# Attention and spectral filter on one Trainium2 core: scratch for eight filter rows, a pair turned in two steps, and inverse-transform visits of two places

## The chip, the cores and the metric

The kernel runs on one core of a Trainium2 chip (trn2), all in float32. The metric is the device time of one execution in microseconds (us). Times are given as the median of several executions; in addition one execution was taken by the hardware profiler, and all views of the profile are of that one.

A core has TensorE (matrix products; PE in the profile, its weight loads PEld), VectorE (DVE), ScalarE (ACT), GpSimd (POOL) and SyncE (SP), which here only issues transfers. Each engine works through its own instructions in order. Matmuls write to PSUM, which has eight banks; VectorE and ScalarE empty it. The profile counts a float32 matmul as two records and a transpose as one.

## The reference

The input is an image batch `x` of shape (2, 128, 64, 64). A first layer (group norm, a neighbourhood attention and two small products) adds to it. The second layer, where the change lies, is this:

```python
t = _to_tokens(x)                      # (2, 4096, 128)
t = t + _L1_attn_ref(_ln_t(t))
t = t + _L1_ffn_ref(_ln_t(t), sigma, phi, M_u, M_phi_plus, M_phi_minus, log_weights, gumbel)

def _L1_attn_ref(q):                   # queries, keys and values are the same
    sim = jnp.einsum('blh,bmh->blm', q, q) * scale
    sim = jnp.where(diag[None, :, :], -1e9, sim)
    return jnp.einsum('blm,bmh->blh', softmax(sim), q)

def _stu_conv(phi, u, n):              # causal convolution with 16 filters, by Fourier transform
    Vf = jnp.fft.rfft(phi, n=n, axis=0)
    Uf_p = jnp.fft.rfft(u, n=n, axis=1)
    Uf_m = jnp.fft.rfft(u * sgn3, n=n, axis=1)
    U_plus = jnp.fft.irfft(Vf[None, :, :, None] * Uf_p[:, :, None, :], n=n, axis=1)[:, :sl]
    U_minus = jnp.fft.irfft(Vf[None, :, :, None] * Uf_m[:, :, None, :], n=n, axis=1)[:, :sl]
    return (U_plus, U_minus * sgn[None, :, None, None])
```

The two convolved signals are mixed by 128 x 128 matrices for each filter (`M_phi_plus`, `M_phi_minus`), and a product with three lags of the input (`M_u`) is added. Four branches over the first 1, 1/2, 1/4 and 1/8 of the tokens are weighted by a softmax of `log_weights` and `gumbel`.

## The kernel before

One program does everything, in stages that follow each other on TensorE. The first layer takes about 350 us. Then comes the attention of batch 0 (to about 750 us) and that of batch 1 (to 1139 us), what is left of the forward transform (to about 1190 us), the spectral stage (to 1945 us), and a tail that finishes batch 1.

**Attention** (`attention(b, fill)`). The 4096 tokens lie in eight chunks of 512. As queries and keys are the same, the scores are symmetric, and the loop runs over the 36 pairs (a, c) with a <= c. Each pair has four steps `j`. `weights` (L926 or L935 for the scores, L931 or L942 for the exponentials on ScalarE) makes a block of the next pair; on a pair of equal chunks VectorE masks the diagonal first (L940), and the blocks under it are got by transposes (L948, copied at L949). In each step, block `j` of the present pair is multiplied with the tokens: into `other` (L1057), which belongs to chunk c, has one PSUM bank and is added to `xa` by VectorE (L1066), or, where a equals c, into `own` (L984). The transposed block gives chunk a its part: for most pairs the exponentials go to DRAM and come back (L958, L965), VectorE turns them in 32 x 32 squares (L974), and the matmuls onto `own` (L984) follow some steps later out of the list `late`. `pass_on(2)` takes up to two matmuls that are due from this list. The pair (6, 7), the last but one, is turned on TensorE instead, by `turned_here` (L980: four transposes into a bank, copied by VectorE at L981), one block a step, and its matmul is due one step later. When the last part has come, `complete` adds `own` to `xa` (L989) and hands the chunk to the filler.

**The filler** (`fill`). After each step one piece of other work is issued: first from `urgent`, which holds for each finished chunk its normalisation and the first stage of the forward transform (`after`: L1125, VectorE work L1128 to L1137, statistics L183 and L184, L191, transposes L202, products L1176 and L1190, stores L1161 and L1092), then from `steps`; in batch 0 these are `drain`, `branch_weights`, `filters` and `tokens(1)`. A piece that says "not now" lets the next queue run. While seven chunks are done, a step in which all queues are empty or say "not now" takes one group of lag products from `kept` (L1220, six matmul records, its result added by VectorE at L1236). The order on the engines is that of the program from here on (`manual_schedule`), except after the second attention and in the tail, where the framework orders it.

**`filters`** transforms the filters. There are 12 pieces (three row sets, four segments each): L1368 on TensorE, a running sum on ScalarE (L1375) or VectorE (L1377), sum and difference on GpSimd (L1381), and, where the piece has imaginary rows, two negatives on VectorE (L1393, L1394), eight such pairs in all. All are stored to DRAM by GpSimd's queue (L1092), up to two transfers a step. Sums and negatives use `cm[1]` as scratch, the channel-major copy for batch 1, which is not filled yet; the negatives have two places in it, in turn. `tokens(1)`, the last piece, then fills `tok[1]` (L191) and `cm[1]`.

**Spectral stage.** There are 40 groups, 20 for each batch. A group has 32 products of four matmuls with 32 rows each (`project`, L1617, two halves `l` of 16 `k`), into the four banks `acc`. Before `k` = 0 and 8 of each half comes a `burst` for the next group: eight matmuls into four `pc` banks (L1598), each copied to `y` by VectorE or ScalarE (L1603). `mixed_bins` copies `acc` (L1627) and mixes it on GpSimd (L1628 to L1646) into `ob` or `ob_last`. `rest` holds pieces of the inverse transform, which are taken after `k` = 4 and 12. After the 16th group of each batch this is `back`: eight places, each with four transposes (L1669) into a `pc` bank, a copy to `t` on ScalarE (L1670), and one visit later four products with 128 rows (L1656) into another `pc` bank and two additions to `xa` on VectorE (L1662). The `pc` banks are a ring of four, shared with the bursts. After batch 0's last group, `finished(0)` makes its output in nine visits.

**Tail.** For batch 1, `turned` transposes the last bins (L1683, L1684). Then, for each half `h` of the output, the residual is brought into PSUM for two of four banks (L1778), 32-row products with 64 columns are added for both parities (L1698), and the result is copied by ScalarE (L1792) or added to the residual by VectorE (L1790) into `o`, which one transfer sends out (L1707). A bank holds both parities of one half.

Of the kernel before, what the change touches and what calls it, by code (L numbers as in the profile page):

```python
# [88 lines left out]
K2 = Q // 2  # L89
# [13 lines left out]
def kernel(  # L103
# [773 lines left out]
    with ap_:  # L877
# [23 lines left out]
        def attention(b, fill):  # L901
# [135 lines left out]
            for i, (a, c) in enumerate(pairs):  # L1037
                following = pairs[i + 1] if i + 1 < len(pairs) else None
                coming, halves = [], []
                if a != c:  # L1040
                    other = ps_o.tile([P, 512], F32, tag="other", name="other")
                else:
                    owns[a] = ps_o.tile([P, 512], F32, tag="own", name="own", bufs=2)
                for j in range(4):
                    if tt[1] is not None and not ordered:
                        ordered.append(written.enter_context(tc.manual_schedule(engines={engines.PE, engines.DVE, engines.Activation, engines.Pool, engines.SP})))
                    due = late and late[0][0] <= step
                    while following and len(coming) < min(4, j + (2 if j == 0 and a != c and not due else 1)):
                        coming.append(coming_of(*following, len(coming), coming, halves))
                    n = 4 * CHUNKS[a] + j  # L1050
                    turn = lambda v, o: v.rearrange(o, q=4, t=4) if far(a, c) else v
                    if j == 0:
                        pass_on(2)
                    if a == c:
                        onto(owns[a], n, owns[a], es[j], j == 0, a == 7 and j == 3)
                    else:
                        nc.tensor.matmul(  # L1057
                            turn(other, "p (q t j) -> p q t j"), lhsT=tok[b][:, n, :], rhs=es[j],
                            start=(j == 0), stop=(j == 3),
                        )  # L1060
                    if a != c and j == 3:
                        xs, ov = xa[b][:, chunk(c)], other
                        if far(a, c):
                            xs, ov = xs.rearrange("p (t q j) -> p q t j", t=4, q=4), ov.rearrange("p (q t j) -> p q t j", q=4, t=4)
                        if a:
                            nc.vector.tensor_tensor(xs, ov, xs, ALU.add)  # L1066
                        else:
                            nc.vector.tensor_copy(xs, ov)
                    if a != c and not far(a, c):
                        if j == 0:  # L1070
                            here = ep.tile([P, 4, 512], F32, tag="et", name="et", bufs=2)
                        turned_here(here, es, j)
                        late.append((step + 1, a, c, here, j))
                    if j:
                        pass_on(2)
                    fill()
                    step += 1
                es = coming
# [258 lines left out]

        def filters():

            negatives = cm[1][:, 3 * SG * LL : (3 * SG + 4) * LL].rearrange("p (a g c) -> p a g c", a=2, g=2)  # L1340
            ph = {}
            for (hh, e), pn in pns.items():
                at = (2 * hh + e) * LL
# [12 lines left out]

            everything = [(r0, c0 + ri * P, (ri,), P) for r0, c0 in row_tiles for ri in range(2)]
            everything.append((left_row, left_col, (0, 1), 64))
            for r0, c0, parts_, m in everything:
                places = cm[1][:, SG * LL : (3 * SG) * LL].rearrange("p (j e c) -> p j e c", j=SG, e=2)  # L1360
                for j in range(SG):
# [26 lines left out]
                            store(fb[mine], r0, n, ri, s, 1, 1)  # L1388
                    if 1 in parts_:
                        mine = slice(m - n, m)  # L1390
                        fn = negatives[:, j % 2]
                        one, two = sums[mine, 0, :], sums[mine, 1, :]
                        nc.vector.scalar_tensor_tensor(fn[mine, 0, :], one, -1.0, two, ALU.mult, ALU.subtract)  # L1393
                        nc.vector.tensor_tensor(fn[mine, 1, :], two, one, ALU.subtract)  # L1394
                        store(fn[mine], r0, n, 1, s, 1, 0)
# [173 lines left out]
    with ExitStack() as cv:  # L1569
# [77 lines left out]

        def back(b, chunk, places):

            waiting = None  # L1650
            for place in (*places, None):
                if waiting:
                    par, f, t = waiting
                    py = slot().rearrange("p (a q) -> p a q", a=4)
                    for a in range(4):
                        nc.tensor.matmul(py[:, a, :], lhsT=t[:, a, :], rhs=inv[:, 4 * chunk + a, :], start=True, stop=True)  # L1656
                    xv = xa[b][:, par * TH : (par + 1) * TH].rearrange(
                        "p (h x e f c l) -> p x f e l h c", x=NFP, e=2, f=2, c=64, l=2
                    )[:, f // 2, f % 2]
                    for e in range(2):  # L1660
                        pv = py[:, 2 * e : 2 * e + 2].rearrange("p l (h c) -> p l h c", c=64)
                        nc.vector.tensor_tensor(xv[:, e], pv, xv[:, e], ALU.add)  # L1662
                if place:
                    par, f = place
                    t = cp.tile([P, 4, P], F32, tag="t", name="t", bufs=4)
                    pt = slot().rearrange("p (a q) -> p a q", a=4)
                    for a in range(4):
                        src = ob[:, b, chunk, a, par].rearrange("p k (o t) -> p t (k o)", t=FB)
                        nc.tensor.transpose(pt[:, a, :], src[:, FB - 1 - f], ident)  # L1669
                    nc.scalar.copy(t, pt)  # L1670
                    waiting = par, f, t
                    yield True
            yield None

# [58 lines left out]
        with tc.manual_schedule(engines={mybir.EngineType.PE}):  # L1733
# [14 lines left out]
            for i, (b, g) in enumerate(groups):  # L1748
# [3 lines left out]
                for l in range(2):  # L1752
                    for k in range(KF):
                        if following is not None and k % 8 == 0:
                            burst(following, 2 * l + k // 8)
                        project(y, acc, l, k)
                        if rest and k in (4, 12):
                            if next(rest[0], None) is None:
                                rest.pop(0)
                mixed_bins(b, g, acc, nc.vector if final else nc.gpsimd)  # L1760
# [9 lines left out]

        b = NB - 1
        ts = [turned(b, par) for par in range(2)]
        for h in range(2):
            o = cp.tile([P, HQ, 2, 2, FB, 2], F32, tag="o", name="o", bufs=2)
            pys = [(sums(a) if h else slot()).rearrange("p (s f q) -> p s f q", s=2, f=FB) for a in range(4)]
            for a in (0, 2):
                for par in range(2):
                    nc.tensor.matmul(  # L1778
                        alike(pys[a][:, par]), lhsT=ident, rhs=residual(b, par, h, a),
                        start=(par == 0), stop=False, skip_group_check=True,  # L1780
                    )
            for par in range(2):
                for f in range(FB):
                    for a in range(4):
                        last_products(pys[a][:, par], ts[par], h, f, a, bool(a % 2))
            for par in range(2):
                for a in range(4):
                    to = place_of(o, par, a)
                    if a % 2:
                        nc.vector.tensor_tensor(alike(to), alike(pys[a][:, par]), residual(b, par, h, a), ALU.add)  # L1790
                    else:
                        nc.scalar.copy(to, pys[a][:, par])  # L1792
            send(b, h, o)


# [93 lines left out]
```

## Time and profile before

| | |
|---|---|
| median of three executions | 1963.6 us (1962.83 to 1963.72) |
| the profiled execution | 1964.29 us, its span 1962.6 us |
| mean granted TensorE clock in it | 0.989 of full speed |
| instructions | 50,908 |
| moved by DMA | 226.16 MB, mean 115 GB/s |
| L1617, 10,240 matmul records | 638.1 us |
| L1598, 2,560 | 209.3 us |
| L1057 and L926 and L984 | 227.5, 222.5 and 276.9 us |
| L1656, 128 | 18.5 us, VectorE idle before L1662 33.2 us |

Busy time of TensorE is summed over records that overlap, and a record lasts until its end is modelled, so these are not times at full use. "Idle before" is the time that an engine stood still ahead of an instruction, with the instruction or transfer that released it. It costs something only where that engine is the one that sets the end, so the chain of waits has to be read with it. In lists of waits, the columns are who waited, for whom, the total in us, how often, and the longest. In a timeline they are start, length, engine, line, operation, what is written from what, the shape, how many were merged, and in brackets the idle time before. In a table of stretches, the columns are the stretch, its length, the engine's busy time with its instructions, the granted clock, the share of the DMA engines and GB/s.

### The profile page before, as it was taken

The page shows a single profiled execution, that of the slowest core. Times are in us where ns is not written, and L with a number is a line of the kernel's source. Part 1 is how long each engine was busy: PE and PEld are TensorE (multiplying, and loading weights), DVE is VectorE, ACT ScalarE, POOL GpSimd, SP SyncE. Part 2 cuts the span into 40 slices and gives each one's busy share as a digit, 9 for nine tenths or more (in the row PEclk, how much of TensorE's full clock was granted, in tenths as well). Part 3 has the DMA queues.
Part 4 walks back from the last instruction along what each step waited for, and adds up shares of the span by engine and source line. Part 5 has one row for each costly group of instructions (what it writes and reads, how often), then busy time and mean ns, then how long its engine had stood idle before and what let it go on. Part 6 is the DMA issues. An engine that isn't in the chain of part 4 may idle for free.

```text
span 1962.6 us, 50908 instructions
## 1 busy us (share of the span) xinstructions
PE 1898.9 (97%) x20504; PEld 1351.1 (69%) x20504; DVE 955.2 (49%) x3026; ACT 732.2 (37%) x1718; POOL 737.7 (38%) x1209
## 2 busy tenths in 40 slices
PE   6899998999999999999999998999999999999998
PEld 4677776444444444444444446999998999999987
DVE  5799997454554534354544463333333343333332
ACT  2789887323233333332333222322222222222221
POOL 4366885524643335532425331222221121222211
PEclk8999999999999999999999999999999999999999
DMA  4222221767776544877966413222222223222211
GB/s 157 61 61 60 62 61 38 158 182 215 215 204 192 151 121 123 269 209 221 252 199 185 122 53 83 66 68 66 67 68 50 59 74 87 66 68 67 66 39 44
DMA packets 249770, 226.16 MB, mean 115 GB/s; under 512 B 126815, under 2 KB 204655, under 8 KB 242112
## 3 DMA queue, kind: packets, MB, share of 16 engines
q1 hardware_dynamic: 222786, 129.15, 27.2%
q10 hardware_dynamic: 8126, 58.04, 7.6%
q0 software_dynamic: 18624, 35.72, 6.2%
q8 instruction: 163, 2.67, 0.6%
q14 instruction: 71, 0.58, 0.1%
HBM read 131.40 MB, written 91.25 MB: 113 GB/s over the span
## 4 chain that ended last, share of the span: by engine, by line
PE 79%; DVE 6%; POOL 5%; DMA 4%; issue 2%; ACT 2%; SPq 1%; DVEq 0%; POOLq 0%; ACTq 0%
PE acc L1617 29%; PE own L984 11%; PE bank L926 8%; PE other L1057 8%; PE pc L1598 7%; PE bank L349 2%; PE bank L935 2%; PE bank L202 2%; PE bank L559 1%; PE bank L1176 1%; PE bank L1220 1%; DMA et<-eb 1%; ACT p L546 1%; DMA us<-ub 1%; DMA eb<-e 1%
## 5 line engine op out<-in xcount | busy, mean ns | idle before, releaser
L1603 DVE COPY y<-pc 128x512 f32<-128x512 f32 x320 | 206.3, 686 | 346.7 <-PE pc L1598 346.4
L1617 PE MATMUL acc<-y,mpl 32*128 32x256 f32 x5120 | 323.0, 379 | 0.8 <-DVE af L1627 0.8
L1603 ACT COPY y<-pc 128x512 f32<-128x512 f32 x320 | 171.9, 589 | 393.3 <-PE pc L1598 388.7
L1617 PE MATMUL acc<-y,mmi 32*128 32x256 f32 x5120 | 315.1, 375 | 0.0
L1617 PEld LDWEIGHTS acc<-y,mpl 32*128 32x128 f32 x5120 | 289.2, 186 | 7.5 <-DVE af L1627 1.6
L1617 PEld LDWEIGHTS acc<-y,mmi 32*128 32x128 f32 x5120 | 290.7, 185 | 2.9
L1628 POOL TENSOR_TENSOR af<-af 128x512 f32<-128x512 f32 x39 | 49.7, 1275 | 578.2 <-DVE af L1627 506.1
L1057 PE MATMUL other<-e,tok 128*128 128x512 f32 x448 | 227.5, 594 | 2.3 <-DVE xa L1066 2.2
L931 ACT ACTIVATE e<-bank 128x512 f32<-128x512 f32 x216 | 129.2, 599 | 250.6 <-PE bank L926 246.3
L926 PE MATMUL bank<-cm 128*128 128x512 f32 x432 | 222.5, 601 | 0.0
L984 PE MATMUL own<-et,tok 128*128 128x512 f32 x448 | 211.9, 595 | 6.2 <-DVE et L974 3.4
L1598 PE MATMUL pc<-ct,ut 32*128 32x256 f32 x2560 | 209.3, 376 | 2.0 <-DVE y L1603 2.0
L1161 POOL TENSOR_TENSOR ub<-uo 128x256 f32<-128x256 f32 (+1 forms) x176 | 111.5, 668 | 178.8 <-ACT uo L1157 150.8
L1598 PEld LDWEIGHTS pc<-ct,ut 32*128 32x128 f32 x2560 | 170.7, 186 | 7.7 <-DVE y L1603 4.1
L974 DVE STREAM_TRANSPOSE et<-et 128x512 f32<-128x512 f32 x216 | 134.2, 679 | 75.9 <-DMA et<-eb 75.8
L984 PEld LDWEIGHTS own<-et,tok 128*128 128x128 f32 x448 | 84.5, 191 | 113.1 <-issue 91.4
L1057 PEld LDWEIGHTS other<-e,tok 128*128 128x128 f32 x448 | 81.4, 191 | 92.1 <-issue 82.4
L926 PEld LDWEIGHTS bank<-cm 128*128 128x128 f32 x432 | 76.1, 191 | 73.7 <-issue 68.1
L546 ACT ACTIVATE p<-p,mn 128x196 f32<-128x196 f32 x256 | 114.4, 449 | 14.4 <-DVE mn L536 13.7
L1092 POOL DMA_DIRECT2D us<-ub x158 | 107.8, 722 | 12.0 <-DMA us<-ub 7.4
L1157 ACT COPY uo<-bank 128x512 f32<-128x512 f32 (+1 forms) x96 | 45.5, 518 | 97.1 <-PE bank L1176 56.9
L536 DVE CUSTOM_DVE_ANT_0 p<-bank,tab 128x196 f32<-128x196 f32 x256 | 76.5, 354 | 4.9 <-PE bank L523 4.7
(267 smaller groups left out, 2591.4 us busy)
## 6 DMA issues: line engine op xcount, KB each, us to landing
eb<-e ACTq DMA_DIRECT2D x54, 1024.0 KB
et<-eb SPq DMA_DIRECT2D x216, 256.0 KB
ut<-us SPq DMA_DIRECT2D x156, 128.0 KB
us<-ub POOLq DMA_DIRECT2D x54, 256.0 KB, 5.0
vw<-vd SPq DMA_DIRECT2D x256, 49.0 KB
ct<-gs SPq DMA_DIRECT2D x312, 40.0 KB
ct<-gs SPq DMA_DIRECT2D x312, 32.0 KB
vd<-v SPq DMA_DIRECT2D x128, 32.0 KB
```

The costliest lines, as they stand in the source:

```text
L536: nc.vector.tensor_tensor_reduce(t[name + "p"][:, h, :], t[name + "S"][h][:, 0:KEYS], tab[:, ci, h, :], 1.0, 3.0e38, ALU.add, ALU.min, t[n ...
L546: nc.scalar.activation(p, p, AF.Exp, bias=t[name + "mn"][:, h : h + 1], scale=-1.0, accum_out=t["den"][:, u, h : h + 1],)
L926: nc.tensor.matmul(ps.rearrange("p (q t j) -> p q t j", q=4, t=4), lhsT=cm[b][:, n * P : (n + 1) * P], rhs=keys.rearrange("p (t q j) -> p ...
L931: nc.scalar.activation(e, ps.rearrange("p (q t j) -> p q t j", q=4, t=4), AF.Exp, bias=0.0, scale=ASCALE)
L974: in_place(nc.vector.transpose(part, part))
L984: nc.tensor.matmul(out_, lhsT=tok[b][:, n, :], rhs=e, start=first, stop=last, skip_group_check=True)
L1057: nc.tensor.matmul(turn(other, "p (q t j) -> p q t j"), lhsT=tok[b][:, n, :], rhs=es[j], start=(j == 0), stop=(j == 3),)
L1092: by.dma_start(out=to, in_=part)
L1161: adder[sgn].tensor_tensor(ub[:, sgn, 0:n], both[:, 0:n], both[:, n : 2 * n], op)
L1598: nc.tensor.matmul(pcs[j].rearrange("p (g o c) -> p o g c", g=4, o=2)[:, :, at], lhsT=ut[rows_, par, :], rhs=cv_[rows_], start=True, stop= ...
L1603: (nc.scalar.copy if j % 2 else nc.vector.tensor_copy)(y[:, :, :, 4 * kl + j, :], pcs[j].rearrange("p (g x k) -> p k g x", g=4, k=KF))
L1617: nc.tensor.matmul(acc[j][:, 0:256], lhsT=(mmi if l else mpl)[rows_, k, :], rhs=y[rows_, k, 2 * l : 2 * l + 2].rearrange("p s n x -> p (s ...
```

## The change

Four edits in one. The negatives of `filters` get eight places, in `tok[1]` instead of `cm[1]`, taken in turn over all pieces. The pair (6, 7) is turned in its first two steps, two blocks in each, and its matmuls are put on the list accordingly. `back` handles two places in a visit (first the products of the two places before, then the transposes of two new ones), and `rest` is visited after `k` = 4 alone. In the tail, the eight banks are taken at once, a bank holds both halves of one parity, and the 32-row products have 128 columns, both halves in one.

```diff
@@ attention
-                        turned_here(here, es, j)
-                        late.append((step + 1, a, c, here, j))
+                        for m in (2 * j, 2 * j + 1) if j < 2 else ():
+                            turned_here(here, es, m)
+                            late.append((step + 1, a, c, here, m))
@@ filters
-            negatives = cm[1][:, 3 * SG * LL : (3 * SG + 4) * LL].rearrange("p (a g c) -> p a g c", a=2, g=2)
+            negatives = tok[1].rearrange("p n c -> p (n c)").rearrange("p (a g c) -> p a g c", g=2, c=LL)
+            taken = 0
-                        fn = negatives[:, j % 2]
+                        fn = negatives[:, taken % negatives.shape[1]]
+                        taken += 1
@@ back
-            waiting = None
-            for place in (*places, None):
-                if waiting:
-                    par, f, t = waiting
+            waiting = []
+            for now_ in (*(places[i : i + 2] for i in range(0, len(places), 2)), []):
+                for par, f, t in waiting:
...
-                if place:
-                    par, f = place
+                waiting = []
+                for par, f in now_:
...
-                    waiting = par, f, t
+                    waiting.append((par, f, t))
+                if now_:
                     yield True
@@ the groups
-                        if rest and k in (4, 12):
+                        if rest and k == 4:
@@ the tail
+        pys = [[sums(a) if par else slot() for a in range(4)] for par in range(2)]
+        half = [[[py.rearrange("p (f h c) -> p h f c", f=FB, h=2)[:, h] for h in range(2)] for py in of] for of in pys]
+        for a in (0, 2):
+            for par in range(2):
+                for h in range(2):
+                    nc.tensor.matmul(
+                        alike(half[par][a][h]), lhsT=ident, rhs=residual(b, par, h, a),
+                        start=(h == 0), stop=False, skip_group_check=True,
+                    )
+        for par in range(2):
+            for f in range(FB):
+                for a in range(4):
+                    rows_ = slice(32 * a, 32 * a + 32)
+                    nc.tensor.matmul(
+                        pys[par][a][:, f * CQ : (f + 1) * CQ], lhsT=ts[par][rows_, f, :],
+                        rhs=inv[rows_, K2 // BC * 4, :], start=bool(a % 2), stop=True, skip_group_check=True,
+                    )
         for h in range(2):
             o = cp.tile([P, HQ, 2, 2, FB, 2], F32, tag="o", name="o", bufs=2)
-            pys = [(sums(a) if h else slot()).rearrange("p (s f q) -> p s f q", s=2, f=FB) for a in range(4)]
-            for a in (0, 2):
-                for par in range(2):
-                    nc.tensor.matmul(
-                        alike(pys[a][:, par]), lhsT=ident, rhs=residual(b, par, h, a),
-                        start=(par == 0), stop=False, skip_group_check=True,
-                    )
-            for par in range(2):
-                for f in range(FB):
-                    for a in range(4):
-                        last_products(pys[a][:, par], ts[par], h, f, a, bool(a % 2))
...
-                        nc.vector.tensor_tensor(alike(to), alike(pys[a][:, par]), residual(b, par, h, a), ALU.add)
+                        nc.vector.tensor_tensor(alike(to), alike(half[par][a][h]), residual(b, par, h, a), ALU.add)
                     else:
-                        nc.scalar.copy(to, pys[a][:, par])
+                        nc.scalar.copy(to, half[par][a][h])
             send(b, h, o)
```

## The prediction

> **What bounds the kernel now.** I read the page's engine shares first, then its chain of waits.
>
> ```profile
> PE 1898.9 (97%) x20504; PEld 1351.1 (69%) x20504; DVE 955.2 (49%) x3026; ACT 732.2 (37%) x1718; POOL 737.7 (38%) x1209
> PE 79%; DVE 6%; POOL 5%; DMA 4%; issue 2%; ACT 2%; SPq 1%; DVEq 0%; POOLq 0%; ACTq 0%
> ```
>
> TensorE is busy for 97% of the span and is 79% of the chain. So from the first attention on (350 us) the end moves by what TensorE waits and by what it issues. Next the list of waits, cut to TensorE as the waiter from 380 us on (total us, times, longest):
>
> ```profile
> PE own L984 <- DVE et L974: 3.4, 2, 3.0
> ...
> PE own L984 <- DVE et L981: 2.8, 2, 1.4
> PE other L1057 <- DVE xa L1066: 2.2, 1, 2.2
> ...
> PE pc L1669 <- POOL ob L1641: 1.9, 2, 1.0
> ```
>
> The 2.8 and the 2.2 lie on lines that the change touches.
>
> **Negatives in eight places.** Timelines of VectorE and TensorE around 508 us (start, length, line, wait before it in brackets):
>
> ```profile
> 502.18 0.69 DVE L1377 TENSOR_TENSOR cm<-bank,cm 128x512 f32<-128x512 f32 x1 [4.67 <-PE bank L1368]
> 509.05 0.42 DVE L1393 SCALAR_TENSOR_TENSOR cm<-cm 128x256 f32<-128x256 f32 x1 [6.18 <-DMA gs<-cm]
> 509.39 0.42 DVE L1394 TENSOR_TENSOR cm<-cm 128x256 f32<-128x256 f32 x1
> 509.73 0.68 DVE L1066 TENSOR_TENSOR xa<-other,xa 128x512 f32<-128x512 f32 x1
> ```
> ```profile
> 506.40 1.88 PE L984 MATMUL own<-et,tok 128*128 128x512 f32 x4
> 510.46 1.13 PE L1057 MATMUL other<-e,tok 128*128 128x512 f32 x2 [2.18 <-DVE xa L1066]
> ```
>
> L1393 wants a place whose store is still on its way. Behind it in VectorE's queue stands L1066, which empties the only `other` bank, and TensorE stands still for 2.18 us. The loop makes eight negatives (L1393 x8), so with eight places none is reused. L1393 can start at 502.9, L1066 when the pair's last L1057 ends (503.99 in the timeline), four us before TensorE asks. Next late would be L948, which transposes the exponentials of L942: VectorE's L940 can then run at the end of L935 (506.6), L942 takes 0.60, so they are there at 507.5 and are asked for at 509.9. The two other waits of L1393 for its stores (0.65 and 1.55 us) hold nobody up. **2.2 us.**
>
> The new places lie in `tok[1]`, so the token pieces must wait for the stores to leave. The first write of `tok` (L191) is at 555.04, the last store is issued at 542.36, and stores land in 1.9 to 9.3 us (4.2 in the median): cost 0. SP's queue isn't touched; POOL's three stores of the fourth place come some 4 us sooner.
>
> **Pair (6, 7).** The TensorE timeline, at the end of the first batch's pair:
>
> ```profile
> 738.46 0.60 PE L980 MATMUL bank<-ident,e 128*128 128x128 f32 x4
> 738.89 1.02 PE L984 MATMUL own<-et,tok 128*128 128x512 f32 x2
> 741.34 1.12 PE L984 MATMUL own<-et,tok 128*128 128x512 f32 x2 [1.42 <-DVE et L981]
> ```
>
> The fourth block is turned in step 3; its copy L981 stands in VectorE's queue behind a normalisation's statistics (737.54 to 739.3), L940, L949 and L1066, and TensorE waits 1.42 us at 741.34, and again 1.42 at 1131.62. Afterwards all four are turned in steps 0 and 1. Moving 0.44 us transposes and 0.86 us matmuls along the timeline puts the last turn at 733.4 to 733.8, its copy at 734.1 to 734.8, and its matmul at 738.4. No wait is left there: **2 x 1.42 = 2.8 us.**
>
> What is pushed back: the copy of the second block (0.6) goes ahead of L940 of step 1, which TensorE's L935 releases only at 732.0, so 0.1 at most. L1125 comes 1.7 later (two more L984 before it), its VectorE chain ends at 738.2 instead of 736.5, and the next reader (L948 of step 3, 739.4) has the exponentials of step 2 at 738.9. L989 now stands before the statistics and waits some 0.7 for TensorE; L940 of step 3 slips to 741.9 and its reader, the last matmul of (7, 7), comes after 747. No DMA moves.
>
> There is a second effect. `complete(6)` comes two steps earlier, so the filler takes one more group of L1220 (six matmuls, 2.58 us) inside each attention. Both groups (5.16 us) are missing after the second attention (1139 to 1190), where they filled the time between L1125 (1147.1) and L202 (1163.4). Their work is done earlier, so the sum is 0 if TensorE stays busy there. L202 would be asked for at 1158.2; its input is VectorE's L191, now done at 1158.1 but behind L1236 copies of just these groups; without them about 1157.4. Close, so 0, with 5.2 as the other end.
>
> **Inverse transform.** The chain of waits in order of time: a half group with a visit of `back`, and one without.
>
> ```profile
> 1905.49 2.16 PE acc L1617 x40
> 1907.65 1.09 PE pc L1656 x8
> 1908.74 0.48 PE pc L1669 x4
> 1909.21 1.51 PE acc L1617 x24
> 1910.72 0.86 PE pc L1598 x16
> ...
> 1917.60 3.45 PE acc L1617 x64
> 1921.06 0.86 PE pc L1598 x16
> ```
>
> The first five add up to 6.10, the last two to 4.31: a visit costs 1.79. Of that, work is 8 products at 0.112 (the spacing of their starts once running) and 4 transposes at 0.12: 1.38. The other 0.41 is the change from 32-row to 128-row matmuls and back. Each `back` has nine visits and afterwards five with the same work: 4 x 0.41 x 2 batches = **3.3 us**. `finished` keeps nine visits, only spread over twice as many groups. The waits for POOL at each first visit (1.0 each) stay; the last visit stays in the same group (4+4+1 before, 2+2+1 after).
>
> Its cover: a double visit takes all four `pc` slots, and the next burst wants all four. From the visit's start, ScalarE's second copy L1670 would run from about 3.2 to 3.8 (before: one copy at 1.73; then one place's products 0.89, transposes 0.48 and one copy more), VectorE's four L1662 from 1.2 to 2.9. The burst comes at 4.35 (before: 1904.45 - 1901.48 = 2.97, plus 1.38). Half a us is left: cost 0.
>
> One rule of the Trainium skill speaks against this part. First the rows (length, TensorE busy, granted clock):
>
> ```profile
> 1861.24:1864.65 3.41, 2.40 (x20) 1.00 0.21 50
> 1864.65:1868.06 3.41, 3.41 (x36) 0.50 0.00 0
> ```
>
> After the POOL wait at 1862 the clock is halved for 3.41 us, which costs 1.7; after the same wait at 1485 it is not. "TensorE: Matmul & The Clock Gate" (Part 4) says that PE transposes don't count as busy. Then four more transposes (0.48) behind each first wait add idle time, and a halving at 1485 is likely: +1.7, a sum of 7.6 instead of 9.3. If they count, they rather save the one at 1862: 11.0. No row here separates them; I take neither and keep both for the range.
>
> **The tail.** ScalarE's and SP's rows:
>
> ```profile
> 1953.10 1.94 ACT L1792 COPY o<-pc 128x256 f32<-128x256 f32 x4 [3.14 <-PE pc L1698]
> 1955.15 2.10 SPq L1707 DMA_DIRECT2D out_dram<-o  x2
> ```
>
> Before, L1698 fills the four banks of one half with 64 records from 1951.07 (0.028 each), and only then do the copies start. Afterwards the banks belong to one parity, with 32 records of 128 columns. A record costs between 0.028 (as with 64 columns) and 0.037 (between that and L1617's 0.054 at 256); the nearer row, and weight loads that don't change, speak for 0.028. The copies start at 1951.07 + 0.9 + 0.1 = 1952.1 (1952.4 at the other end); the second parity is done before the copies get to it. So the first output DMA is issued 1.0 earlier (0.7), and as both keep the DMA engines full from 1956 to 1961 (401 to 459 GB/s), the end follows. **0.95 us.** The eight residual matmuls (L1778) stay.
>
> **Sum.** 2.2 + 2.8 + 3.3 + 0.95 = 9.3 us off the profiled execution's 1964.3 (span 1962.6): 1955.0, span 1953.3. The median, 1963.6, is 0.7 lower: **1954.3**. A measurement of this kernel tells 0.2%, or 3.9 us, from no change.
>
> **Rivals.**
> - *The missing filler.* The stage from 1139 to 1190 is set by its VectorE, POOL and store chain, not by TensorE. For: TensorE waits 2.0 for it at 1181.4. Against: until 1174 it never waits there. Then 5.2 come back: 1959.5. Chance 0.12.
> - *A later DMA takes the gain.* At 914.3 TensorE waits 3.0 us for a transfer behind L974. If DMA sets that moment, the 3.6 gained before it (2.2 + 1.4) go into that wait: 1957.9. Against: those transfers are issued when TensorE's own steps let them. Chance 0.08.
> - *The four slots are not free in time* (the slower side). Place: the burst after each of the eight double visits that carry copies. If copies end more than 0.5 us later than I place them, TensorE idles; a 1 us idle can halve the clock as at 1862. At 1.0 wait each and four halvings: 8 + 6.8 = 14.8 lost, 1969.1. It decides for slower from a wait of 1.2 each without halvings. Against: all 32 L1662 last 0.415 to 0.426 us, whatever POOL does. Chance 0.05.
> - *The change does nothing where it aims*, as when `tok[1]` brings a wait that stands in for the old: 2 to 3 us less gain, 1957. Chance 0.1.
>
> **How the numbers follow.** The forecast, with its clock cases (1952.6 to 1956.0), has 0.65. Range: from 1951.8, both clock luck and a little more, to 1959.5, which takes in the filler and the DMA case. Faster by over 0.2% (below 1959.7): the forecast, the third small case, the DMA case and most of the filler's, 0.87. Within: the rest of the filler's and sums of two cases, 0.08. Slower: 0.05.
>
> **What would show it.** No TensorE wait at 508 for L1066 and none for L981; nine visits become five, x16 and x8 records in one piece of the chain; half groups with a double visit of 7.5 us (4.31 + 2 x 1.38 + 0.41); no wait of L1598 for L1670; the tail's first copy 2.0 us after L1698 starts becoming 1.0. Wrong if L1220's time shows up as idle TensorE between 1139 and 1190, or if bursts wait on `t`.

## The result, and the profile after

| | before | after |
|---|---|---|
| median (five executions of each in all) | 1962.83 us | 1951.74 us |
| range | 1960.16 to 1963.72 | 1946.84 to 1954.66 |
| profiled execution, its span | 1964.29, 1962.6 us | 1954.66, 1952.8 us |
| granted clock, instructions | 0.989, 50,908 | 0.990, 50,772 |

The ratio of the times is 0.9945, with a 95% interval of 0.9927 to 0.9962: faster by about 11 us (7.5 to 14), where 9.3 were forecast. The profiled execution gained 9.6. The forecast was 1954.3 us with a range from 1951.8, so the median lies at the fast edge of that range. One execution of the kernel before that was timed beside the experiments took 2202.2 us at a granted clock of 0.847, and is in none of the ratios.

First the page of the kernel after: the engine shares, and the shares of the chain of waits by engine. Line numbers after the change are two or three higher in the spectral stage (L1620 is the former L1617, L1601 the burst L1598, L1606 its copies L1603, L1630 the copies of `acc` L1627; L1658 the products, L1664 the additions, L1671 the transposes and L1672 the copies of `back`, formerly L1656, L1662, L1669 and L1670). In the tail L1781 is the former L1778, L1701 the former L1698, L1789 has the new products, L1801 is the former L1792 and L1710 the former L1707. L1379, L1396 and L1397 are the former L1377, L1393 and L1394; L1221 is L1220, L1237 is L1236 and L1158 is L1157.

```profile
PE 1891.0 (97%) x20440; PEld 1347.5 (69%) x20440; DVE 956.0 (49%) x3026; ACT 731.3 (37%) x1718; POOL 737.7 (38%) x1209
PE 84%; DVE 5%; POOL 4%; DMA 2%; issue 1%; ACT 1%; SPq 0%; ACTq 0%; DVEq 0%; POOLq 0%
```

TensorE has 64 records less (the tail), is still the bound, and its share of the chain has grown from 79% to 84%: waits have gone. The list of waits of the kernel after, TensorE as the waiter from 380 us on (total us, times, longest), says which.

```profile
PE bank L202 <- ACT uo L1158: 3.4, 3, 2.4
PE own L984 <- DVE et L974: 3.2, 1, 3.2
PE pc L1686 <- POOL ob_last L1649: 2.1, 1, 2.1
PE pc L1671 <- POOL ob L1644: 2.0, 2, 1.0
```

Neither L1057's wait for L1066 nor L984's waits for L981 are in the list any more. The waits for GpSimd at the first visits stay (L1671 in `back`, L1686 in `finished`), as does one for a transfer behind L974. The largest, of L202 between the attentions and the spectral stage, has grown from 3.0 to 3.4.

To see where the time went, the two traces were cut at the same instructions: at the last `own` matmul of each attention, and at the first and the last product of the spectral stage (us; in brackets how long TensorE ran on a halved clock there):

```
                         before            after         difference
first layer              348.21 (23.9)     347.88 (20.5)   -0.33
attention, batch 0       400.70 (0)        398.72 (0)      -1.98
attention, batch 1       390.28 (3.4)      391.88 (6.8)    +1.60
between them and spectrum 65.85 (3.4)       61.13 (3.4)    -4.72
spectral stage           739.72 (6.8)      734.95 (3.4)    -4.77
tail                      17.81             18.25          +0.44
```

A window of halved clock lasts 3.4 us and costs at most half of that, 1.7 us, an estimate from its length and its clock of 0.50. One more of them in the second attention and one less in the spectral stage about cancel. The tail, which should have gained 0.95, has lost 0.44.

### The profile page after: what moved, and what is told of

The parts are those of the page before. It is cut to its first block, busy times and chain, and to the rows that moved or that the text cites. A ratio compares the mean times of both kernels' runs of the same rounds, so it can differ in the third digit from the quotient of the medians.

```text
span 1952.8 us, 50772 instructions
## 1 busy us (share of the span) xinstructions
PE 1891.0 (97%) x20440; PEld 1347.5 (69%) x20440; DVE 956.0 (49%) x3026; ACT 731.3 (37%) x1718; POOL 737.7 (38%) x1209
## 4 chain that ended last, share of the span: by engine, by line
PE 84%; DVE 5%; POOL 4%; DMA 2%; issue 1%; ACT 1%; SPq 0%; ACTq 0%; DVEq 0%; POOLq 0%
PE acc L1620 29%; PE own L984 12%; PE other L1057 9%; PE bank L926 9%; PE pc L1601 7%; PE bank L349 2%; PE bank L935 2%; PE bank L559 2%; PE bank L202 2%; PE bank L1177 1%; PE bank L1221 1%; PE bank L523 1%; ACT p L546 1%; PE po L581 1%; PE pc L1658 1%
## 5 line engine op out<-in xcount | busy, mean ns | idle before, releaser
L1606 DVE COPY y<-pc 128x512 f32<-128x512 f32 x320 | 206.2, 686 | 348.6 <-PE pc L1601 348.3
L1606 ACT COPY y<-pc 128x512 f32<-128x512 f32 x320 | 171.8, 589 | 402.5 <-PE pc L1601 396.9
L1620 PE MATMUL acc<-y,mpl 32*128 32x256 f32 x5120 | 321.6, 379 | 0.8 <-DVE af L1630 0.8
L1620 PE MATMUL acc<-y,mmi 32*128 32x256 f32 x5120 | 313.1, 375 | 0.0
L1620 PEld LDWEIGHTS acc<-y,mpl 32*128 32x128 f32 x5120 | 289.4, 186 | 7.3 <-DVE af L1630 1.7
L1620 PEld LDWEIGHTS acc<-y,mmi 32*128 32x128 f32 x5120 | 290.4, 185 | 2.6
L1057 PE MATMUL other<-e,tok 128*128 128x512 f32 x448 | 227.5, 594 | 0.2
L984 PE MATMUL own<-et,tok 128*128 128x512 f32 x448 | 212.1, 598 | 3.3 <-DVE et L974 3.2
L1601 PE MATMUL pc<-ct,ut 32*128 32x256 f32 x2560 | 208.3, 376 | 2.0 <-DVE y L1606 2.0
L1601 PEld LDWEIGHTS pc<-ct,ut 32*128 32x128 f32 x2560 | 170.1, 185 | 7.6 <-DVE y L1606 4.1
L974 DVE STREAM_TRANSPOSE et<-et 128x512 f32<-128x512 f32 x216 | 134.2, 678 | 70.9 <-DMA et<-eb 70.8
L984 PEld LDWEIGHTS own<-et,tok 128*128 128x128 f32 x448 | 85.7, 192 | 111.2 <-issue 96.1
L1057 PEld LDWEIGHTS other<-e,tok 128*128 128x128 f32 x448 | 81.5, 191 | 89.6 <-issue 82.1
L1158 ACT COPY uo<-bank 128x512 f32<-128x512 f32 (+1 forms) x96 | 45.4, 517 | 96.9 <-PE bank L1177 55.2
L1630 DVE COPY af<-acc 128x256 f32<-128x256 f32 x80 | 30.3, 420 | 104.6 <-PE acc L1620 104.6
```

The source lines that it names most:

```text
L974: in_place(nc.vector.transpose(part, part))
L984: nc.tensor.matmul(out_, lhsT=tok[b][:, n, :], rhs=e, start=first, stop=last, skip_group_check=True)
L1057: nc.tensor.matmul(turn(other, "p (q t j) -> p q t j"), lhsT=tok[b][:, n, :], rhs=es[j], start=(j == 0), stop=(j == 3),)
L1601: nc.tensor.matmul(pcs[j].rearrange("p (g o c) -> p o g c", g=4, o=2)[:, :, at], lhsT=ut[rows_, par, :], rhs=cv_[rows_], start=True, stop= ...
L1606: (nc.scalar.copy if j % 2 else nc.vector.tensor_copy)(y[:, :, :, 4 * kl + j, :], pcs[j].rearrange("p (g x k) -> p k g x", g=4, k=KF))
L1620: nc.tensor.matmul(acc[j][:, 0:256], lhsT=(mmi if l else mpl)[rows_, k, :], rhs=y[rows_, k, 2 * l : 2 * l + 2].rearrange("p s n x -> p (s ...
```

## The experiments

Each is an edit of the kernel after, and the diffs are against it. Those with a ratio were timed beside the kernel before on their own chip; the others are single executions, read by their stages.

**The tail as it was.**

```diff
-        pys = [[sums(a) if par else slot() for a in range(4)] for par in range(2)]
...
         for h in range(2):
             o = cp.tile([P, HQ, 2, 2, FB, 2], F32, tag="o", name="o", bufs=2)
+            pys = [(sums(a) if h else slot()).rearrange("p (s f q) -> p s f q", s=2, f=FB) for a in range(4)]
...
+                        last_products(pys[a][:, par], ts[par], h, f, a, bool(a % 2))
```

> The changed kernel with the tail of before (banks by half, 64-column products), the other three edits kept. Theory (the tail edit lost a little, because the copies run parity by parity and the first output DMA waits for the sixth of eight copies): from the last product of the last group to the end 17.8 us, as before (17.8), against 18.2 in the changed kernel; median 0.4 us under the changed kernel's. Rival (the forecast's: the tail edit gains 0.95, and what is lost is lost elsewhere): this stretch is 19 us or more and the median 0.95 above.

The tail measured 17.81 us, as in the kernel before. The time was 1954.22 us, ratio 0.9958 (0.9942 to 0.9974); an effect of 0.44 us can't be told in it, but the stage settles it: the tail's part of the change is a loss. The reason is in the timelines. First the kernel after (start, length, engine, line, operation, what is written from what, shape, how many merged, idle time before):

```profile
1940.88 1.17 PE L1789 MATMUL pc<-inv,t 32*128 32x128 f32 x32
...
1942.07 1.92 ACT L1801 COPY o<-pc 128x256 f32<-128x256 f32 x4 [2.31 <-PE pc L1789]
1943.79 1.96 ACT L1801 COPY o<-acc 128x256 f32<-128x256 f32 x4
1945.41 0.83 SPq L1710 DMA_DIRECT2D out_dram<-o  x2
```

Then the same stretch with the former tail:

```profile
1939.54 2.01 PE L1701 MATMUL pc<-inv,t 32*128 32x64 f32 x64
...
1943.63 2.10 SPq L1710 DMA_DIRECT2D out_dram<-o  x2
```

The copies start 1.19 us after the first product instead of 2.03, near the 1.0 of the forecast. But after the change four of them in a row read `pc`, then four read `acc`. A bank now holds one parity of both halves, so this is the order by parity, not by half: the framework, which orders this stage, has put the four copies of the first parity first, on ScalarE and on VectorE. The first half of the output is complete only when the second parity is under way, and its transfer starts 4.53 us after the first product, against 4.09. The second transfer follows 0.46 us later, where it was 1.7 before.

**The tail's copies by half.** The order of VectorE and ScalarE is taken from the framework.

```diff
+        with tc.manual_schedule(engines={mybir.EngineType.DVE, mybir.EngineType.Activation}):
-        for h in range(2):
+            for h in range(2):
...
```

> The changed kernel, with the tail's copies held in the program's order on VectorE and ScalarE: all of half 0, then all of half 1. Theory: the first output DMA is issued 3.1 to 3.2 us after the first 128-column product (4.5 in the changed kernel, 4.1 before), and as the two transfers fill the DMA engines from then on, the end follows: last group to end 16.8 us instead of 18.2, median 1.4 lower. Rival (the end is set by the second transfer, issued at the same time in both): 18.2, no gain.

The timeline of this kernel:

```profile
1936.59 1.17 PE L1789 MATMUL pc<-inv,t 32*128 32x128 f32 x32
...
1938.67 1.03 ACT L1802 COPY o<-acc 128x256 f32<-128x256 f32 x2
...
1939.82 2.09 SPq L1710 DMA_DIRECT2D out_dram<-o  x2
```

The copies now alternate, two from `pc` and, as shown, two from `acc`, and the first transfer starts 3.23 us after the first product, 0.85 earlier than in the kernel before. The tail lasts 16.96 us: 1.29 less than after, 0.85 less than before. The time was 1952.15 us, ratio 0.9941 (0.9924 to 0.9958), in which this again can't be told. So nearly all of the forecast's 0.95 was there to be had, and the order of the copies had taken it.

**Visits begun only when the mixing is done.** The first visit of each piece of the inverse transform waits for GpSimd's last mixing; here visits begin half a group later.

```diff
-                        if rest and k == 4:
+                        if rest and k == 4 and (l or g % (BC // KG) and g):
```

> The changed kernel, without the visit in the first half of a group that follows directly on the one whose bins the inverse transform reads, so that GpSimd is done mixing them. Theory (these waits are the largest left in the spectral stage, and they bring the halved clock): TensorE's waits there (1.0, 2.1 and 1.0 us) are gone, the first four transposes stand 0.12 apart instead of 0.42 (0.9 each time), and the halvings after them (1.7 each, one in the changed profile) are gone: 5.9 us, with the halving 7.6; span 1945 to 1947. Rival (the waits only move to the later visit or to the bursts): span within 2 us of the changed kernel's 1952.8.

The time was 1944.21 us, ratio 0.9901 (0.9875 to 0.9927). This is the whole list of its waits, TensorE as the waiter from 1200 us on:

```profile
PE pc L1686 <- DVE ob_last L1649: 0.9, 1, 0.9
PE acc L1620 <- ACT af L1630: 0.8, 1, 0.8
PE acc L1781 <- DVE af L1630: 0.4, 1, 0.4
```

No wait for GpSimd is left, and no window of halved clock falls into the stage, which lasts 726.35 us instead of 734.95. That is 8.6 less (6.9 at equal clock, as the kernel after has one halved window there), more than the expected 7.6; part of the surplus is that the visits of `finished` cost less at these places (40.7 us for eight, from burst to burst, instead of 41.8).

**Both of these.**

> The two edits above together: the tail's copies by half and no visit while GpSimd mixes. Theory: they add up, 7.3 to 9 us under the changed kernel, span 1944 to 1945.5. Rival: only the tail's 1.4, 1951.4.

1942.97 us (1942.63 to 1943.28), ratio 0.9894 (0.9872 to 0.9916), tail 16.92 and spectral stage 726.34 us: the two edits add up in their stages. This is the lowest median of the study; against the kernel with the later visits alone it can't be told in the ratio.

**One place a visit.** The `back` of the kernel before, with visits at `k` = 4 and 12.

```diff
-            for now_ in (*(places[i : i + 2] for i in range(0, len(places), 2)), []):
+            for place in (*places, None):
...
-                        if rest and k == 4:
+                        if rest and k in (4, 12):
```

> The changed kernel with the inverse transform of before: one place a visit, visits after k = 4 and 12. Theory (each visit costs a change of matmul mode and back, 0.41 us, and four visits a batch are saved): half groups with a visit of 6.10 us instead of 7.47 with two places, and the spectral stage, from its first product to its last, 3.3 us longer than the changed kernel's 735.0 (1.7 more or less for each halving of the clock that differs from the changed kernel's one). Rival (visits cost nothing beyond their matmuls; the gain in this stage was the clock): stage within 1 us of 735.0 at the same number of halvings.

The stage measured 737.62 us against 734.95, at 3.4 us of halved clock in each: 2.67 instead of 3.3. (The kernel before, whose code in this stage is the same as here, took 739.72 with one halved window more, 0.4 longer at equal clock; why is not shown.) Adding up the stretches from burst to burst (the prediction's half groups) finds the difference. For the two `back` pieces alone they differ by 3.3 us (1.63 and, without a halved window, 1.67), the forecast's figure. But the eight visits of `finished` that follow its first take 41.8 us after the change and 41.2 here. A half group with a visit is 0.35 to 0.4 us longer when it is the first quarter of a group: 7.87 instead of 7.47 for `back`, 5.40 instead of 5.05 for `finished`. Without a visit the first quarter is only 0.08 longer (4.40 instead of 4.32), although the group's own products wait for the copies of `acc` (L1630) with and without one. With visits at 4 and 12, every fourth falls there; at 4 alone, every second. The quarter alone doesn't decide: in the kernel with visits begun when the mixing is done, the visits of `finished` in first quarters take 5.13. There these are the visits with `a0` = 0 (rows 0 to 63), in the kernel after those with `a0` = 2 (rows 64 to 127). Why the extra time comes with these stays open. The forecast left `finished` at nothing ("only spread over twice as many groups").

**The visit right before a burst.** This tests the cover of half a microsecond that the forecast put on the ring of four `pc` banks.

```diff
-                        if rest and k == 4:
+                        if rest and k == 7:
```

> The changed kernel with the visit after k = 7, directly ahead of a burst, so that the burst wants the four banks at once. In the changed kernel the second copy to t ends 3.7 us after the visit's first product, and 0.65 before the burst. Theory: the cover was the three projects between, 1.3 us; without it each of the eight visits with transposes makes the burst wait 0.6 us for ScalarE's second copy, 5 us in the stage, and the waits are shown at L1601 for L1672. Rival (the ring of four banks is no limit at all): no such waits, stage within 1 us.

The stage took 744.25 us without any halved clock, some 11 us more than the kernel after at equal clock. A visit of `back` with both its parts and the plain stretch behind it, together, take 7.77 + 4.75 to 4.80 us, against 7.47 or 7.87 + 4.32 after: 0.55 more on average. The rows of one such burst in this kernel:

```profile
1504.63 1.07 ACT L1672 COPY t<-pc 128x512 f32<-128x512 f32 x2 [5.23 <-PE pc L1671]
1504.95 0.61 PEld L1601 LDWEIGHTS pc<-ct,ut 32*128 32x128 f32 x6
...
1505.76 0.51 PEld L1601 LDWEIGHTS pc<-ct,ut 32*128 32x128 f32 x9 [0.20 <-ACT t L1672]
```

The burst starts, stops until the second copy L1672 has ended (1505.70) and then goes on. With three `k` of products less in between, the ring is not free in time. Most of the cost, however, lies in `finished`, which the expectation hadn't counted: a visit there fills two of the four banks, both emptied by VectorE alone (L1725), and its eight visits cost 8.8 us more. The list of waits has eight for it:

```profile
PE pc L1601 <- DVE o L1725: 3.1, 8, 0.6
```

In these 3.1 of the 8.8 us TensorE stands still; in the rest it is shown as busy, and what takes it stays open. The first visits no longer wait for GpSimd in `back`, and only 0.8 us in `finished`, so the 11 us are what is left after that gain.

**The two edits, and only `back` right before a burst.**

```diff
-                        if rest and k == 4 and (l or g % (BC // KG) and g):
+                        if rest and k == rest[0][0] and (l or g % (BC // KG) and g):
...
+                    rest.append((7, back(b, g * KG // BC, [(par, f) for par in range(2) for f in range(FB)])))
...
+                    rest.append((4, finished(b)))
```

> The kernel with both edits (visits begun once the mixing is done, and the tail's copies in written order), and the visits of the inverse transform moved from k = 4 to k = 7, right before a burst; the visits of the output of batch 0 stay at k = 4. Theory (two of the three changes between 32-row and 128-row matmuls become one, and the ring of four is ready in time for all but some 0.5 us): each of the eight double visits costs about 0.27 us less, so the spectral stage goes from 726.3 to about 724.2 and the time from 1943.0 to about 1941. Rival (the burst's wait for its four banks is worse once the visits come later against the mixing): bursts after double visits last over 1.6 us instead of 1.3, and the stage is 2 us or more longer than 726.3.

A miss: the stage grew to 731.97 us, 5.6 more than with visits at `k` = 4, and the time was 1947.35 us, ratio 0.9899 (0.9875 to 0.9923), which can't be told from the 0.9894 of the kernel with both edits; the stage can. The 0.27 us that I expected to save per visit came from a wrong reading of the run before. I had cut the stretches at the first burst record, and a record of a burst that had come out of step stood there among the products, as in this part of this kernel's chain:

```profile
1513.72 1.65 PE pc L1601 x14
1515.37 0.02 PE acc L1620 x3
1515.39 0.20 PE pc L1601
```

The burst's last record (1515.39) comes after three records of the next products. Cut where the burst really begins, a visit saves nothing by standing next to a burst, and costs the same 0.55 as in the run before.

**Two places for the negatives**, in the new memory and with the new turn.

```diff
-                        fn = negatives[:, taken % negatives.shape[1]]
+                        fn = negatives[:, taken % 2]
```

> The changed kernel with two places for the negatives, in tok[1]. Theory (what counts is that no place is used a second time while its store is under way, not where it lies): TensorE's wait for L1066 near 505 us is back with 2.2 us, and the first attention takes 401 to 401.6 us instead of 398.7. Rival (it was the place in cm[1], or the store's timing): no wait, 398.7.

In this kernel's timeline the old stall is back:

```profile
510.28 0.42 DVE L1396 SCALAR_TENSOR_TENSOR tok<-cm 128x256 f32<-128x256 f32 x1 [7.07 <-DMA gs<-tok]
...
510.96 0.69 DVE L1066 TENSOR_TENSOR xa<-other,xa 128x512 f32<-128x512 f32 x1
...
511.70 1.86 PE L1057 MATMUL other<-e,tok 128*128 128x512 f32 x2 [3.08 <-DVE xa L1066]
```

The negative waits for its store, L1066 stands behind it, and TensorE waits 3.08 us for L1066. A window of halved clock follows (3.4 us long), and the first attention takes 403.72 instead of 398.72 us. The mechanism is the forecast's. The size is 0.9 us above the 2.2 expected: counted from the start of the attention, the store let L1396 go 0.9 us later than in the kernel before (161.73 instead of 160.84). The attention is 2.1 us above the expected 401.6, of which the halved window explains up to 1.7.

**One block a step for the pair (6, 7)**, as before the change, with all else kept.

```diff
-                        for m in (2 * j, 2 * j + 1) if j < 2 else ():
+                        for m in (j,):
```

> The kernel after, with the pair (6, 7) turned one block a step again and its matmuls due as before; the eight places, the visits and the tail stay. Theory (the pair's part is worth the two waits for L981, and the two groups of lag products only change their stage): TensorE waits for L981 some 1.4 us again in each attention, two groups of L1221 (2.58 us each) go back from the attentions into the stage between the attentions and the spectral one. So each attention changes by -2.58 + 1.4 to 1.7, that is about -1.0 (398.7 becomes 397.7 for the first), the stage between grows from 61.1 to about 65.8, and the whole is 2.8 to 3.4 us longer in the profile at equal clock. Rival (the missing groups were a loss that the waits' removal only made good): the stage between grows by less than 3 us and the whole is within 1 us of the kernel after.

In this kernel's list of waits L984's for L981 are back:

```profile
PE own L984 <- DVE et L981: 2.8, 2, 1.4
```

The first attention took 397.84 us (0.9 less, as a group of lag products went out of it), and the stage between attentions and spectrum 67.38, or 65.7 without the one additional halved window, which is 4.5 more than after. Both are as expected; the pair's part is worth about 3 us.

**Four groups of lag products early instead of two.** If the stage between has no room for TensorE's work to be missing, taking still more out of it gains nothing.

```diff
-                    next(kept[0], None)
+                    for _ in range(2):
+                        next(kept[0], None)
```

> The changed kernel, with two groups of lag products in each free step near the end of an attention instead of one: four in each attention, two more than in the changed kernel, so that four of them (10.3 us) are missing after the second attention as well. Theory: between the second attention and the first project TensorE has only 1.6 us of slack left ahead of L202 of the last but one chunk, so most of the missing 10.3 us becomes idle TensorE: 7 to 9 us of new waits there, time 7 to 9 us up. Rival (the stage has room, as it had for the first two groups): no new waits, same time.

The first attention grew by 5.16 us, as it must with two groups more. The stage between went from 61.13 to 55.54 us, with 4.5 us more of idle TensorE, where 7 to 9 were expected. Its waits between 1100 and 1210 us show a new one:

```profile
PE bank L202 <- DVE z L191: 2.7, 1, 2.7
```

So the rival of the missing filler names the right wait, L202 for L191. But it arises only when twice as much is taken out, and even then half of what goes is gained.

## Why the prediction was right, and where it was wrong

**Negatives (2.2 forecast).** Right. The timelines of the kernel after around 505 us; first VectorE:

```profile
502.58 0.42 DVE L1396 SCALAR_TENSOR_TENSOR tok<-cm 128x256 f32<-128x256 f32 x1
...
503.71 0.69 DVE L1066 TENSOR_TENSOR xa<-other,xa 128x512 f32<-128x512 f32 x1 [0.36 <-PE other L1057]
```

L1396 runs right behind its sum (L1379, 501.86 to 502.55), and L1066 waits for nothing but the matmuls it reads. On TensorE, the time from one piece of `filters` (L1370) to the next fell from 14.12 us (500.94 to 515.06) to 11.26 (500.62 to 511.88), 2.86 less. The wait of 2.18 brought 2.45: the profile counts a wait from the modelled end of the matmuls ahead, and here L1057 starts 0.17 us before that end when it needn't wait; the second record behind the wait came another 0.10 late. A wait of 0.19 at an L948 (513.94) brought the other 0.41.

**Pair (6, 7) (2.8).** Right, and the forecast's doubt about the filler was settled on the side it took. TensorE's timeline of the kernel after:

```profile
727.26 1.04 PE L980 MATMUL bank<-ident,e 128*128 128x128 f32 x8
...
737.42 2.74 PE L1221 MATMUL bank<-zc,mu 128*128 128x512 f32 x6
```

Eight records of transposes in a step (the same again at 729.75), no wait in front of any L984, and at 737.42 the additional group of lag products. The first attention shortened by 2.0 us: 2.86 gained by the negatives and 1.7 by the pair, 2.58 paid for that group. The stage between attentions and spectrum shortened by 4.72 of the 5.16 that its two groups had taken; its idle time grew by 0.5, most of it in one wait of L202 for L1158 (2.4 instead of 2.0). What the rival would have cost at the earlier L202 stayed away because L191 ended 1.6 us before it asked.

**The DMA that might take the gain.** The wait for a transfer behind L974 is 3.17 us after and 3.02 before, so it did not take the gain ahead of it. In the executions of the other kernels it varied between 1.4 and 6.0, which is why the times of single executions say little here.

**Inverse transform (3.3).** The mechanism was right, and the term was 0.6 too large, by the run with one place a visit. The chain of waits of the kernel after, over one visit and the start of the next:

```profile
1888.71 2.16 PE acc L1620 x40
1890.87 1.98 PE pc L1658 x16
1892.85 0.96 PE pc L1671 x8
1893.81 1.51 PE acc L1620 x24
1895.32 0.86 PE pc L1601 x16
...
1900.50 2.56 PE acc L1620 x40
```

The first five make 7.47 us, against 7.5 forecast, and no burst waits; the second copy to `t` ends 0.65 us before the next burst, where the forecast had half a microsecond of cover. The run with visits at `k` = 7 showed that the ring does hold up the burst once the products between are gone. The last row shows what the forecast overlooked: the same 40 records take 2.56 us instead of 2.16 when the visit falls into the first quarter of a group. For `back` that happens as often as before the change, for `finished` twice as often, and that is most of the missing 0.6.

**The tail (0.95).** Wrong in sign. The step that failed is "So the first output DMA is issued 1.0 earlier (0.7)". It took the copies to keep their order by half. Their start was right, but the order was not in the program's hands, and the first transfer was issued 0.44 later. With the order by half written down, the tail gained 0.85.

**The sum.** The terms as measured are 2.9 for the negatives, about 3 for the pair, 2.7 for the visits and -0.4 for the tail: 8.2, against 9.3 forecast and 9.6 found between the two profiled executions. What is left was not forecast. It lies in the first layer (0.3), in the second attention (1.0: an L984 no longer waits 0.35 us for L974, and the additional halved window cost 1.3 us, not 1.7) and in the spectral stage (the 0.4 named above); why is not shown. The forecast was near in part by luck: the over-sized terms of the visits and the tail were made good by waits that brought more than their own length and by this remainder.

**The clock rule.** The forecast weighed a rule of the Trainium skill ("TensorE: Matmul & The Clock Gate", Part 4): if transposes don't count as busy in the same way as matmuls, more of them behind a wait would halve the clock more often. That stays open: the wait of 1.0 us at each first visit of `back` was followed by a halved window at neither, one or both of the two places, in executions of kernels whose code there is the same. With eight transposes behind the wait it was so at 6 of 12 places, with four at 1 of 4. That is too few to tell. When the waits went, no halved window was left in the stage.

## What to carry to other kernels

When buffers are regrouped so that a product can serve two outputs, look at who orders the readers afterwards: an engine that starts earlier ends nothing earlier if its work is dealt out by the new grouping rather than by the transfer that waits for it. Larger visits between tightly scheduled products save the changes between tile shapes, as long as the ring of buffers has recovered before its next user; count the time from the last copy to the next use for every user of the ring, not only the one that was changed. And before making such visits larger, see whether the first one waits for its input at all: starting it half a group later was worth more here (8.6 us, or 6.9 at equal clock) than making it larger (2.7).

## What was unexpected of the hardware

- The scatter of one program's times, 1946.84 to 1954.66 us, has its counterpart in part in windows of halved TensorE clock: the fastest of the five executions had a granted clock of 0.993, the others 0.989 to 0.991 (though among these the time doesn't follow the clock). Kernels with the same first layer spent 10.2 us of it so in one profile (343.79 us long) and 20.5 in another (347.88). A wait as short as 1.0 us can be followed by such a window, as at 1473.7 us in the kernel with its tail copies by half, where TensorE is busy for 2.43 of the 3.5 us around the wait and is granted 0.58 of its clock over the next 3.5, but it doesn't always follow.
- A burst that stalled for one bank left, as I read the records, TensorE's four groups of 32 rows out of step: single burst records come after the first records of the next products, as in the chain of the kernel with `back` right before a burst. It shifts the place at which a stretch seems to begin, and misled one expectation here.
